# Layer 1's cross attention keeps x in SBUF for GEGLU; three tags of small tiles become one; two follower sweeps start earlier

## The chip, the cores and the metric

The program runs on one core of one Trainium2 chip. The metric is the device time of one execution in microseconds (us), lower is better. A core has five instruction streams that matter here: PE (the matmul engine; PEld are its weight loads), DVE (vector), ACT (activations), POOL (GpSimd) and SP, whose stream issues every DMA of this kernel. Each stream runs in its own order, and semaphores join them. SP's stream is one queue: an instruction on it that waits holds all that stand behind it.

## The reference

Four transformer layers run over x (32 batches of 112 rows and 256 columns) with a shared context (32 batches of 375 rows and 256 columns), in fp32:

```python
x = L0(x, ctx)   # cross attention, 16 query heads of 64 on 4 key heads, no residual
x = L1(x, ctx)   # quantised self attention, quantised cross attention, GEGLU
x = L2(x, ctx)   # cross attention with 16 heads of 64, ReLU feed-forward
x = L3(ctx, x)   # causal self attention, cross attention, ReLU feed-forward
```

Layer 1 is what the change is about. Its blocks each read the normalised x and add to x:

```python
h2 = _ln(x, ln2_g, ln2_b)
x = _attn(h2, context, a2_wq, a2_wk, a2_wv, a2_wo, a2_bo, d_q2, d_k2, d_v2, d_w2) + x
h3 = _ln(x, ln3_g, ln3_b)
hg = h3 @ ff_w1 + ff_b1
a, g = jnp.split(hg, 2, axis=-1)
x = a * jax.nn.gelu(g, approximate=False) @ ff_w2 + ff_b2 + x
```

In `_attn`, queries, keys and values are rounded to 8-bit steps, and so are the softmax's probabilities (16 heads of 16 columns).

## The kernel before

**Sweeps.** The nine blocks are sweeps over all 32 batches: l0x, l1s (self attention of layer 1), l1x (its cross attention), l1f (its GEGLU), l2x, l2f, l3s, l3x, l3f. Batches go in pairs (GB = 2). A sweep is a list of units (one per batch, or one per pair for a feed-forward), and a unit is a list of slots: l1x has 8 slots for a batch (two heads each), l1f 8 for a pair (one eighth of the hidden columns each). Work that prepares a unit (loads, norms, projections) is a list of atoms, each with a lead: so many slots of its own sweep ahead (LEAD, L79). Work that follows a slot (normalising the probabilities, their transpose, the values' matmul, the residual) comes so many slots behind it (LAGS, L67).

**Which sweeps run together.** PAIRS (L29) puts l1s beside l0x, l1f beside l1x, l3s beside l2f and l3f beside l3x. `order` (L1338) gives every slot a place on one axis, from which all slots are sorted. The second sweep of a pair starts `off` later:

```python
off = max(GB * dur + self.DELAY[s] * dur, done + self.GAP - t0) if q else 0.0
```

`dur` is the pair's nominal length of a batch (SPAN), `done` the place where the pair before ends. With DELAY = 3 l1s runs 5 batches behind l0x. The next pair starts at once when l0x's slots are through, so that l1x runs beside the last batches of l1s; l1f starts GAP = 30 units after l1s's last slot, some 9 batches behind l1x. l2x starts when l1f's slots are through. So the stages of the kernel's first half are: l0x alone, l0x with l1s, l1x with the rest of l1s, l1x with l1f, the rest of l1f alone, l2x.

**Order of instructions.** The Python above issues the work in that order with priorities; the Tile framework's scheduler then fixes the order on each engine, and takes the tiles' buffers from the free slots of their tags (BUFS, L64). A tag with `bufs=11` has 11 slots as large as its largest tile. An instruction whose tile finds no free slot waits for the last reader of an older one.

**x between sweeps.** `load_x` (L380) and `store_x` (L388) hand x over. Where `beside` (L373) is true, the later sweep of a pair takes the SBUF tile of the earlier one. For l1x and l1f it is not, since both stand in AGAIN (L378). Of every batch, l1x loads x (for the norm), loads it again for the residual (L1216), stores it to HBM (L396), and l1f loads it (L385), loads it again for its residual (L1294), and stores it: six DMAs of 112 KB on SP's queue.

**The small tiles.** Tag ki (6 slots of 1,504 bytes a partition) holds l1's rounding tiles (`fkq`, L893) and the rounded keys; ot (7 of 1,792) the attention outputs split in two parts, the rounded queries and the feed-forwards' hidden parts (L1271); pp2 (4 of 1,792) the four-head probabilities (L620), their transposes (L1185) and the masked queries of `queries_apart` (L884).

**The path of l1x's probabilities.** Score matmuls (L1111), row maxima (DVE, L606), exponentials (ACT, L612), reciprocal (DVE, L646), rounding (POOL and DVE, L213), clipping (DVE, L657), a DMA transpose issued from SP (L1130) four times a batch, then the matmuls with the values (PE, L1075) and the projection. The same sweep computes values of layer 2 ahead of time and stores them with four DMAs a batch (L502).

Of the kernel before, what the change touches and what calls it, by code (L numbers as in the profile page):

```python
# [8 lines left out]
F32 = mybir.dt.float32  # L9
# [51 lines left out]

class Kern:

    BUFS = dict(w=8, x=11, xh=4, ki=6, s1=9, sm=32, ot=7, pp2=4, k3=11, h=3, qs=2, k6=5)  # L64
    PBUFS = dict(sc=3, ps1=4, acc=1)

    LAGS = dict(  # L67
# [11 lines left out]
    LEAD = dict(  # L79
        l0x=dict(load=11, stats=10, apply=6, cload=11, cstats=8, cut=8, ctrans=5, q=4, k=[2, -2], v=-1),  # L80
        l1s=dict(load=5, stats=5, apply=3, q=2, k=2, v=1),
        l1x=dict(load=17, stats=12, apply=10, cload=14, cut=14, q=8, apart=[2, -1], k=4, v=-1, v2=[-2, -4, -6, -7], again=-7),
        l1f=dict(load=13, stats=11, apply=10, gate=2, gelu=1, again=-3),
        l2x=dict(load=10, stats=7, apply=6, cload=11, cut=7, q=4, k=[1, 1], v=0, vload=2),
        l2f=dict(load=6, stats=5, apply=3),
        l3s=dict(load=10, stats=8, apply=7, q=7, qload=3, k=6, v=3, c2=4, k2=1, v2=1),
# [288 lines left out]
        return any(self.sweeps[i : i + 2] == list(p) for p in PAIRS) and self.sweeps[i] not in self.AGAIN  # L375


    AGAIN = ("l1x", "l1f")  # L378

    def load_x(self, s, b):  # L380
        i = self.sweeps.index(s)
# [235 lines left out]
    def softmax4(self, sc, scale=None):  # L617

        nc = self.nc
        p = self.t([S, 4, S], F32, "pp2")  # L620
        sm = self.t([S, 4], F32, "sm")
        nm = self.t([S, 4], F32, "sm")
        nc.vector.tensor_reduce(nm, sc, AX.X, ALU.max, negate=True)
        if self.turn("exp4") == 1:
            nc.vector.tensor_tensor(p, sc, nm.unsqueeze(2).to_broadcast([S, 4, S]), ALU.add)
            nc.scalar.activation(p, p, AF.Exp, scale=1.0 if scale is None else scale)
            nc.vector.tensor_reduce(sm, p, AX.X, ALU.add)
            return p, sm
# [98 lines left out]
    def unit64(self, s, b0, i, qd, gb, W, g, cx, wd, wq, wk, wv, gqa, gkv, gvec, bvec):  # L727
# [33 lines left out]
        def mk(m):  # L761
            z = {}

            def a():
                qs = g["q", qd]
                scs = []
                for j in range(2):
                    sc = self.ps([S, 512], "sc")
                    scs.append(sc)
                    hd = 2 * m + j  # L770
                    kk = kv["k", qd // 2][:, qd % 2, :] if gqa else kv["k", m][:, j, :]
                    for q in range(2):
                        nc.tensor.matmul(sc[:, :TE], qs[:, hd, q, bs], kk, start=q == 0, stop=q == 1)  # L773
                z["p"], z["sm"] = self.softmax(scs, T)

            def b():
                if not gqa:
                    st["pt", m] = self.t([TB, 2, 3 * S], F32, "k3")
                elif m == 0:
                    pt = self.t([TB, 2, 2, 3 * S], F32, "k6")  # L780
                    st["pt"], st["pt", 0], st["pt", 1] = pt, pt[:, 0], pt[:, 1]
                self.transpose_p(z["p"], st["pt", m])

            def c():
                if m == 0:
                    return
                vq = kv["v"]
                av = self.ps([128, 2, S])
                for mm in range(1 if gqa else 2):
                    for a in range(3):  # L790
                        ta = slice(a * S, (a + 1) * S)
                        for j in range(2):
                            hd = qd if gqa else 2 * mm + j
                            o = av[64 * j : 64 * j + 64]
                            nc.tensor.matmul(  # L795
                                o if gqa else o[:, mm, :],
                                vq[:, a, hd * 64 : hd * 64 + 64],
                                st["pt"][:, :, j, ta] if gqa else st["pt", mm][:, j, ta],
                                start=a == 0,
                                stop=a == 2,  # L800
                            )
                ot = st["ot"] = self.t([128, 2, 2, S], F32R, "ot")
                self.copy("ohi", ot[:, 0], av)
                nc.vector.tensor_tensor(ot[:, 1], av, ot[:, 0].bitcast(F32), ALU.subtract)

            return Slot(a, lambda: self.normalise(z["p"], self.recip(z["sm"], 2), 2, T), b, c)
# [74 lines left out]

    def queries_apart(self, i, c, bs):

        t = self.t([128, 8, S], BF16, "pp2")  # L884
        self.nc.gpsimd.tensor_tensor(
            t,
            i[:, c, bs].unsqueeze(1).to_broadcast([128, 8, S]),
            self.own.unsqueeze(2).to_broadcast([128, 8, S]),
            ALU.mult,
        )  # L890
        return t

    def fkq(self, ps, inv, shape):  # L893

        nc = self.nc
        p = shape[0]
        f = self.t(shape, F32, "ki")
        self.scale("fk", f, ps, inv[:p], MAGIC)
        self.eng("clip").tensor_scalar(f, f, MAGIC + 127.0, MAGIC - 128.0, ALU.min, ALU.max)
        return f  # L900

    def qk_atoms(self, lead, w, src, W, isq, quant, prm, put, tag=None, keep=None, apart=False):
# [4 lines left out]
        def half(c):  # L907
            if quant and c == 0:
                both = isq and not apart
                z["i"] = self.t([128, 2, 2, W] if both else [128, 2, W], BF16, "ot" if isq else "ki")  # L910
            pq = self.ps([128, W])
            for k in range(2):
                self.mm3(pq, lambda i: w()[:, k, i, c * 128 : (c + 1) * 128], lambda i: src()(k, i), k == 0, k == 1)
# [91 lines left out]
    def unit16(self, s, b0, i, gb, g, wd, quant, self_attn, qb, kb, vb, dl, gvec, bvec):  # L1005
# [54 lines left out]
        def av(heads, pt, first, octets, ahead=True):  # L1060
# [21 lines left out]
                        )  # L1082
            if octets:
                if octets[0] == 0:
                    st["ot"] = self.t([128, 2, 2, S], F32R, "ot")
                oc = slice(octets[0], octets[-1] + 1)
                hi, lo = st["ot"][:, 0, oc, :], st["ot"][:, 1, oc, :]
                o = o[:, : len(octets), :]
                if quant:
                    self.scale("ohi", hi, o, dl["so"])  # L1090
                    nc.vector.scalar_tensor_tensor(lo, o, dl["so"], hi.bitcast(F32), ALU.mult, ALU.subtract)
                else:
                    bi = vb[:, octets[0] : octets[0] + 1]
                    self.shift("ohi", hi, o, bi)
                    nc.vector.scalar_tensor_tensor(lo, o, bi, hi.bitcast(F32), ALU.add, ALU.subtract)
# [52 lines left out]
        def quad(qd):  # L1148
# [28 lines left out]
            def b():  # L1177
# [4 lines left out]
                pst = self.ps([128, 4, S])  # L1182
                for j in range(4):
                    nc.tensor.transpose(pst[:S, j, :], z["p"][:, j, :], self.ident[:S, :S])
                z["pt"] = self.t([S, 4, S], F32, "pp2")  # L1185
                self.copy("copy", z["pt"], pst[:S])

            def c():
# [34 lines left out]
    def unitff(self, s, b0, gb, wd, gvec, bvec, b1, glu):  # L1223
# [33 lines left out]
        def mk(c):  # L1257
            z = {}

            def a():  # L1260
# [7 lines left out]
                    z["uu"] = uu  # L1268
                    return
                self.shift("relu", uu, pf, b1[:, c : c + 1], AF.Relu)  # L1270
                ul = z["ul"] = self.t([128, 2, W], F32R, "ot")  # L1271
                self.split(uu, ul[:, 0, :], ul[:, 1, :], ("upper", "lower"))

            def b():
# [85 lines left out]
        ev.sort(key=lambda e: e[:4])  # L1360
        return [(e[4], e[2], e[5]) for e in ev]

    DELAY = dict(l1s=3, l1f=5, l3s=3, l3f=3)
    GAP = 30.0
    PAUSE = 4
    OVER = dict(l2x=0.0, l3x=34.0)

# [232 lines left out]
```

## Time and profile before

| | us |
|---|---|
| three runs | 4955.44, 4955.54, 4960.33 (median 4955.54) |
| the profiled execution | 4969.08, of which the span of its instructions is 4967.3 |
| PE busy in the span | 4502.3 (91%) |
| DVE, ACT, POOL busy | 3625.6, 3409.2, 2112.1 |
| x loaded from HBM between sweeps (`x<-xd`) | 224 DMAs of 112 KB |
| x stored to HBM between sweeps (`xd<-x`) | 160 DMAs of 112 KB |

A row of a window below gives the stretch, its length, and then for PE, PEld, DVE, ACT and POOL the busy time and in brackets the number of instructions; after them the granted PE clock (1.00 is full), the mean busy share of the 16 DMA engines, and GB/s. Rows of waits give who waited for whom, the sum, how often, and the longest. Rows of a timeline give the start, the duration, the engine (SPq is SP's queue), the line, the operation, out<-in, and how many were merged. Line numbers are those of the kernel before.

### The profile page before, as it was taken

What the parts mean: (1) busy time and instruction counts of PE and PEld (TensorE: products, weight loads), DVE (VectorE), ACT (ScalarE), POOL (GpSimd) and SP (SyncE); (2) the same over time, 40 slices, a digit from 0 to 9 for tenths busy, and PEclk for the clock granted to TensorE, in tenths of its full rate; (3) what the DMA queues carried; (4) which work ended last, traced back from release to release, by engine and by line L of the source; (5) the groups of instructions that cost most, each with busy time, mean ns of one, the idle gap of its engine ahead of it and who ended that gap; (6) DMA issues with size and microseconds to landing.
All of it is one profiled execution on the core that took longest, in us unless ns stands there. A gap on an engine that the chain in (4) does not pass through costs nothing. (4 is left out here: it accounts for less than half of the span.)

```text
span 4967.3 us, 111690 instructions
## 1 busy us (share of the span) xinstructions
PE 4502.3 (91%) x37824; PEld 4010.3 (81%) x37824; DVE 3625.6 (73%) x9806; ACT 3409.2 (69%) x10644; POOL 2112.1 (43%) x3674
## 2 busy tenths in 40 slices
PE   5999999997778888888999999998998986899999
PEld 5888888886667777777999999997888886788878
DVE  4788888888887777776688888886555554677776
ACT  4788888887777766775577777774544544677776
POOL 4455555555443333332233333334333333566665
PEclk9999999999889999999999999999999998899999
DMA  4433333335666667667355555543656657666663
GB/s 102 124 85 86 84 80 88 86 87 127 135 141 134 138 128 135 129 143 143 110 142 143 142 142 143 143 128 108 196 172 198 189 182 212 174 160 165 160 165 85
DMA packets 585414, 674.53 MB, mean 136 GB/s; under 512 B 318688, under 2 KB 495056, under 8 KB 584656
## 3 DMA queue, kind: packets, MB, share of 16 engines
q1 hardware_dynamic: 584848, 667.40, 53.5%
q8 instruction: 305, 5.00, 0.4%
q14 instruction: 261, 2.14, 0.1%
HBM read 323.55 MB, written 173.02 MB: 100 GB/s over the span
## 5 line engine op out<-in xcount | busy, mean ns | idle before, releaser
L217 POOL TENSOR_SCALAR k<-k,sm 112x375 f32<-112x375 f32 (+1 forms) x1536 | 931.8, 619 | 1025.2 <-DVE sm L646 453.9
L200 ACT ACTIVATE k<-ps 125x336 f32<-125x336 f32 (+4 forms) x2005 | 912.8, 468 | 416.1 <-PE ps L237 190.1
L606 DVE TENSOR_REDUCE sm<-sc 112x1 f32<-112x375 f32 x1792 | 941.7, 539 | 151.8 <-PE sc L773 87.2
L612 ACT ACTIVATE k<-sc,sm 112x375 f32<-112x375 f32 x1536 | 879.5, 578 | 116.0 <-DVE sm L606 97.4
L664 PE MATMUL ps<-ident,k 112*125 112x112 f32 x4608 | 737.5, 277 | 19.8 <-issue 4.1
L664 PEld LDWEIGHTS ps<-ident,k 112*125 112x125 f32 x4608 | 649.9, 190 | 78.8 <-issue 41.8
L773 PE MATMUL sc<-k,qs 128*112 128x376 f32 x2048 | 540.0, 356 | 18.5 <-ACT k L612 8.3
L235 PE MATMUL ps<-w,k 128*125 128x256 f32 (+2 forms) x1344 | 435.6, 324 | 32.0 <-ACT k L612 17.9
L235 PE MATMUL ps<-h,w 128*128 128x224 f32 x1408 | 411.9, 300 | 44.0 <-DVE h L202 17.2
L695 DVE TENSOR_TENSOR k<-ps,k 64x376 fp32r<-64x376 f32 x640 | 350.0, 547 | 121.3 <-ACT k L200 106.0
L236 PE MATMUL ps<-h,w 128*128 128x224 f32 x1408 | 397.3, 284 | 0.7 <-DVE h L231 0.3
L237 PE MATMUL ps<-h,w 128*128 128x224 f32 x1408 | 395.0, 283 | 0.0
L236 PE MATMUL ps<-w,k 128*125 128x256 f32 (+2 forms) x1344 | 393.1, 292 | 0.0
L202 DVE COPY k<-ps 125x336 f32<-125x336 f32 (+2 forms) x619 | 289.0, 467 | 141.5 <-PE ps L237 65.2
L237 PE MATMUL ps<-w,k 128*125 128x256 f32 (+2 forms) x1344 | 391.9, 292 | 0.0
L235 PE MATMUL ps<-k,w 128*128 128x376 f32 x896 | 343.2, 383 | 37.2 <-DMA k<-cd 25.4
L213 POOL TENSOR_SCALAR k<-k,sm 112x375 f32<-112x375 f32 x256 | 164.5, 643 | 467.0 <-DVE sm L646 287.8
L795 PE MATMUL ps<-k,k 125*64 125x112 f32 (+1 forms) x4608 | 349.8, 296 | 3.7 <-DVE k L202 1.6
L773 PEld LDWEIGHTS sc<-k,qs 128*112 128x112 f32 x2048 | 304.4, 177 | 47.3 <-ACT k L612 23.5
L235 PEld LDWEIGHTS ps<-h,w 128*128 128x128 f32 x1408 | 275.0, 199 | 70.9 <-issue 28.9
L235 PEld LDWEIGHTS ps<-w,k 128*125 128x125 f32 (+2 forms) x1344 | 266.9, 199 | 72.7 <-ACT k L612 29.3
L612 ACT ACTIVATION_READ_ACCUMULATOR k<-sc,sm 112x1 f32 x1536 | 322.5, 210 | 0.0
(213 smaller groups left out, 12623.3 us busy)
## 6 DMA issues: line engine op xcount, KB each, us to landing
qs<-h SPq DMA_DIRECT2D x512, 224.0 KB
k<-k SPq DMA_DIRECT2D x192, 376.0 KB
k<-cd SPq DMA_DIRECT2D x64, 752.0 KB
vd<-k SPq DMA_DIRECT2D x128, 375.0 KB
k<-vd SPq DMA_DIRECT2D x128, 375.0 KB
qs<-dq_l3s SPq DMA_DIRECT2D x256, 112.0 KB
qs<-dq_l3x SPq DMA_DIRECT2D x256, 112.0 KB
x<-xd SPq DMA_DIRECT2D x224, 112.0 KB
```

Source lines behind the costliest of these rows:

```text
L200: self.nc.scalar.activation(out, in_, AF.Identity)
L202: self.nc.vector.tensor_copy(out, in_)
L217: self.nc.gpsimd.tensor_scalar(out, in_, by, 1.0, ALU.mult, ALU.mult)
L235: mm(out, lhs(0), rhs(0), start=start, stop=False)
L236: mm(out, lhs(0), rhs(1), start=False, stop=False)
L237: mm(out, lhs(1), rhs(0), start=False, stop=stop)
L606: nc.vector.tensor_reduce(nms[j], sc[j][:, :n], AX.X, ALU.max, negate=True)
L612: nc.scalar.activation(p[:, j, :n], sc[j][:, :n], AF.Exp, bias=nms[j], scale=1.0 if scale is None else scale, accum_out=sm[:, j : j + 1])
L664: self.nc.tensor.transpose(pst[:TB, a * S : (a + 1) * S], p[:, j, a * TB : (a + 1) * TB], self.ident[:S, :S])
L695: nc.vector.tensor_tensor(ks[o, j, :], pk[r, :TE], ks[r, j, :].bitcast(F32), ALU.subtract)
L773: nc.tensor.matmul(sc[:, :TE], qs[:, hd, q, bs], kk, start=q == 0, stop=q == 1)
L795: nc.tensor.matmul(o if gqa else o[:, mm, :], vq[:, a, hd * 64 : hd * 64 + 64], st["pt"][:, :, j, ta] if gqa else st["pt", mm][:, j, ta], ...
```

## The change

- AGAIN becomes empty. So `beside` is true for l1x and l1f: l1x adds its residual to the tile that it loaded for the norm, does not store x, and l1f takes that tile, adds to it, and stores it for l2x. Two DMAs of x a batch are left in the two sweeps.
- Tag x gets 14 slots for 11. Tags ki (6), ot (7) and pp2 (4) become one tag m with 14 slots of 1,792 bytes.
- l1s's DELAY is 2 for 3, and GAP 5 for 30: by the formula l1s runs 4 batches behind l0x, and l1f 7 batches behind l1x (the first operand of the `max` decides then, 154 units for 200).
- l1x's load of x has a lead of 14 slots for 17, l1f's of 11 for 13.

```diff
-    BUFS = dict(w=8, x=11, xh=4, ki=6, s1=9, sm=32, ot=7, pp2=4, k3=11, h=3, qs=2, k6=5)
+    BUFS = dict(w=8, x=14, xh=4, m=14, s1=9, sm=32, k3=11, h=3, qs=2, k6=5)
...
-        l1x=dict(load=17, stats=12, apply=10, cload=14, cut=14, q=8, apart=[2, -1], k=4, v=-1, v2=[-2, -4, -6, -7], again=-7),
-        l1f=dict(load=13, stats=11, apply=10, gate=2, gelu=1, again=-3),
+        l1x=dict(load=14, stats=12, apply=10, cload=14, cut=14, q=8, apart=[2, -1], k=4, v=-1, v2=[-2, -4, -6, -7], again=-7),
+        l1f=dict(load=11, stats=11, apply=10, gate=2, gelu=1, again=-3),
...
-    AGAIN = ("l1x", "l1f")
+    AGAIN = ()
...
-        p = self.t([S, 4, S], F32, "pp2")
+        p = self.t([S, 4, S], F32, "m")
...
-        f = self.t(shape, F32, "ki")
+        f = self.t(shape, F32, "m")
...
-                    st["ot"] = self.t([128, 2, 2, S], F32R, "ot")
+                    st["ot"] = self.t([128, 2, 2, S], F32R, "m")
...
-    DELAY = dict(l1s=3, l1f=5, l3s=3, l3f=3)
-    GAP = 30.0
+    DELAY = dict(l1s=2, l1f=5, l3s=3, l3f=3)
+    GAP = 5.0
```

The other lines with the tags ki, ot and pp2 (L799, L884, L910, L1185, L1271) change their tag in the same way.

More of the change, by code (lines that the diff above doesn't have):

```diff
@@ L801, in c @@
                             )
-                ot = st["ot"] = self.t([128, 2, 2, S], F32R, "ot")
+                ot = st["ot"] = self.t([128, 2, 2, S], F32R, "m")
                 self.copy("ohi", ot[:, 0], av)
@@ L882, in queries_apart @@
     def queries_apart(self, i, c, bs):
-        t = self.t([128, 8, S], BF16, "pp2")
+        t = self.t([128, 8, S], BF16, "m")
         self.nc.gpsimd.tensor_tensor(
@@ L909, in half @@
                 both = isq and not apart
-                z["i"] = self.t([128, 2, 2, W] if both else [128, 2, W], BF16, "ot" if isq else "ki")
+                z["i"] = self.t([128, 2, 2, W] if both else [128, 2, W], BF16, "m")
             pq = self.ps([128, W])
@@ L1184, in b @@
                     nc.tensor.transpose(pst[:S, j, :], z["p"][:, j, :], self.ident[:S, :S])
-                z["pt"] = self.t([S, 4, S], F32, "pp2")
+                z["pt"] = self.t([S, 4, S], F32, "m")
                 self.copy("copy", z["pt"], pst[:S])
@@ L1270, in a @@
                 self.shift("relu", uu, pf, b1[:, c : c + 1], AF.Relu)
-                ul = z["ul"] = self.t([128, 2, W], F32R, "ot")
+                ul = z["ul"] = self.t([128, 2, W], F32R, "m")
                 self.split(uu, ul[:, 0, :], ul[:, 1, :], ("upper", "lower"))
```

## The prediction

> **What bounds the kernel now.** The page's slices come first: PE is near full in l0x (to some 1150 us) and in l2x (2450 to 3350), and lower in between. So layer 1 is read by windows: l0x with l1s; l1x with the rest of l1s; l1x with l1f; l1f alone; l2x.
>
> ```profile
> span 4967.3 us, 111690 instructions
> PE   5999999997778888888999999998998986899999
> PEclk9999999999889999999999999999999998899999
> ```
>
> ```profile
> 300.00:1100.00 800.00, 775.02 (x6248) 663.34 (x6249) 659.91 (x1910) 697.30 (x2312) 414.02 (x844) 1.00 0.36 84
> 1150.00:1450.00 300.00, 228.53 (x1724) 188.93 (x1724) 260.13 (x702) 214.81 (x660) 134.07 (x248) 0.87 0.65 138
> 1500.00:2300.00 800.00, 694.94 (x5133) 614.98 (x5130) 600.30 (x1675) 558.25 (x1510) 283.61 (x434) 0.94 0.68 135
> 2322.00:2402.00 80.00, 76.64 (x436) 69.41 (x435) 35.16 (x97) 23.47 (x44) 15.93 (x26) 1.00 0.34 90
> 2450.00:3350.00 900.00, 896.34 (x7976) 846.28 (x7974) 738.51 (x1724) 651.86 (x1850) 292.85 (x496) 1.00 0.50 141
> ```
>
> The reader is to see that PE sets the pace in l0x with l1s (97% busy), in l1f alone (96%) and in l2x (99.6%), and no engine does while l1x runs: 76% and 87% for PE, 87% and 75% for DVE. By counts of l1x's score matmuls (L1111, 16 a batch) l1x takes 36.7 us a batch beside l1s (109 in 250 us from 1200) and 36.0 beside l1f (356 in 800 us from 1500). The much different companions leave its pace the same: it is set by something in l1x itself. Its waits from 1500 to 2300, PE's row and then SP's own:
>
> ```profile
> PE ps L1075 <- DMA k<-k: 63.6, 36, 4.7
> ```
>
> ```profile
> SPq L502 <- DVE k L202: 104.0, 37, 8.9
> SPq L385 <- DVE xh L441: 83.4, 21, 9.1
> SPq L385 <- DMA xd<-x: 81.6, 32, 6.2
> SPq L1130 <- POOL k L213: 63.0, 24, 4.1
> ```
>
> PE stands for 63.6 of its 105 idle us before the values' matmuls, until the transposed probabilities land. SP, which issues those transposes, stands 165 us for x alone: until a store of x has landed that the next load reads (81.6), and until the norm frees a slot of tag x (83.4). What that does to the transposes is in SP's timeline:
>
> ```profile
> 1752.56 3.53 SPq L1130 DMA_TRANSPOSE k<-k  x1
> 1756.70 1.00 SPq L552 DMA_DIRECT2D cd<-k  x1
> 1757.83 1.30 SPq L502 DMA_DIRECT2D vd<-k  x1
> 1760.58 10.21 SPq L385 DMA_DIRECT2D x<-xd  x3
> 1770.90 1.48 SPq L1130 DMA_TRANSPOSE k<-k  x1
> 1773.83 0.26 SPq L502 DMA_DIRECT2D vd<-k  x1
> 1774.15 0.32 SPq L385 DMA_DIRECT2D x<-xd  x1
> 1778.28 0.30 SPq L396 DMA_DIRECT2D xd<-x  x1
> 1778.67 1.36 SPq L1130 DMA_TRANSPOSE k<-k  x1
> ```
>
> A transpose that still waits for its data stands 3 to 5 us (1752.56); one whose data lay ready takes 1.4 (1770.90, right behind three loads of x that held the queue for 10.2 us). Going through the window like this, of 89 transposes 35 were short, and 30 of these stood behind loads or stores of x that had held the queue for more than 1 us. Those were late because of x.
>
> **The change part by part.** The sum is made against the profiled execution's 4969.1 us (13.5 above the median of the three runs, 4955.5, and 1.8 above its span) and then taken off the median. The built programs' orders give what is moved.
>
> *GEGLU's tail.* In PE's order 3.94 pairs of l1f stood behind l1x's last score before, and 2.94 after; the first gate comes after 6.1 batches of l1x, not 8.1. Alone, l1f did 248 of its matmuls at L1238 in 80 us (the window from 2322), 64 a pair: 20.6 us a pair, PE full. The pair moves into l1x's stage, where l1x's pace did not depend on its companion and PE is idle 13 to 24%. Taken: -20.6. Bounds: -20.6, and 0 if the moved PE work lengthens l1x as much. The tail is also when l2x's weights arrive; POOL's waits for these DMAs there (L204 on xh) were 4.6, 4.1 and 2.6 us in sum, of which none is counted and 11 kept for the range.
>
> *l1s one batch earlier.* 4.1 batches of l0x stand before its first score, not 5.1. So one batch of l0x changes from running alone to running with l1s: l0x's scores (L773, 32 a batch) were 107 in 100 us alone (29.9 us a batch) and 734 in 800 us with l1s (34.9). Both are PE-bound: +5.0. l1x loses that batch beside it. Counted 0, since l1x's pace did not change with its companion; it could give back up to the same 5.0.
>
> *The queue.* 96 loads and 32 stores of x go: two DMAs of x a batch are left of six. In SP's order from l1x's 41st to its 120th transpose (20 batches), 24 transposes stood directly behind a load and 6 behind a store of x before, and 10 and 0 after. What is late next is each transpose's own data (POOL's L213, 63.0 us in 24) and the store of layer 2's values (104.0, which stays). Bounds on the gain: 0, if those absorb it all, and all of PE's wait, 63.6 us for 22.25 batches, so 2.86 a batch, times the 25.9 batches that now run beside l1f: 74. I take half, 37: a third of the transposes was held by x, but those held were held long (10.2 us above), and the waits on data that remain are of 2 to 4 us and nearly as frequent.
>
> The Trainium skill's page "Perfetto Trace Analysis", section "Identifying the Most-Contended Engine", speaks against this step: DMA is to be judged by HBM utilization. At the 135 GB/s of l1x's window against the 358 a core of its section "Engine Utilization", DMA is far from full, and taking away 14 MB of transfers would be worth nothing; the forecast would then be 37 higher. I go by the queue's rows.
>
> *The clock.* l1x's windows were granted 0.87 and 0.94, the full stages 1.00. Less idle PE may raise it: 31.2 us of PE a batch (694.94 / 22.25) at 0.98 for 0.94 would be 1.3 us less, 33 over 25.9 batches. I count none and keep 33 for the range, because l3x's stage with 92% busy PE also shows only 0.96.
>
> The page "TensorE: Matmul & The Clock Gate", section "What's actually happening", says that the throttled state is the default and that activity releases it. By it fewer stalls before L1075 would pay twice, and part of the 33 would be added.
>
> *The tiles.* x gets room for l1f's lag: a tile lives from 14 slots (1.75 batches) ahead of l1x's pair until 1.25 batches (LAGS, 5 slots) after l1f's pair, 1.75 + 7 + 2 + 1.25 = 12 batches, and there are 14. Tag m loses three slots against the sum of the three, while l1x and l1s fill all of them (11.5 tiles a batch in l1x); layer 3, which used no ki, gains three. The trace names no wait for a slot of ki, ot or pp2 on PE; the nearest is x's own (83.4 us in 21 on SP, 4.0 each). 0 is taken; above, one such wait a batch (104 us) is the slower rival. The order in l2f with l3s and in l3x changes too (equal shares of PE's instructions in order 0.68 and 0.84; l2x's is the same): idle PE there was 10% and 8% of 600 us, and a tenth of it either way is some 11 us, kept for the range. ACT loads its tables twice more (13 to 14 each way, 1.28 us each): 2.6 us, hidden by ACT's 30% idle time.
>
> Sum: -20.6 + 5.0 - 37 = -52.6: 4916.5 for the profiled execution, 4903 for the median.
>
> **The rivals.**
>
> *Only the tail.* The transposes wait for their own data instead: -20.6 + 5.0, 4940. For it: 54 of 89 transposes waited for data anyway. Against it: 30 that did not.
>
> *All of the queue and the clock.* The 74 and the 33 come whole: 5.0 - 20.6 - 74 - 33 = -122.6, 4833. For it: no engine is full in l1x. Against it: DVE is at 75% and in a chain of four engines, and L502's 104 us stay on the queue.
>
> *Slower: too few slots in m.* Keys and queries of l1x hold slots over a batch or two, and the short rounding tiles (L897) queue behind them on ACT, with the exponentials behind those. It decides above 2.0 us a batch (52.6 / 25.9) that reach PE. At one wait of 4.0 us: +104, 5007. For it: 17 slots become 14 just where all three tags are used. Against it: the three tags could not lend to each other, and ACT has no such wait now.
>
> *Nothing changes in time.* The orders differ as described, so the change does what it says; its parts would have to cancel: 4955.
>
> **How the numbers follow.** Forecast 0.52 (its own range 4880 to 4930), only the tail 0.20, all of the queue and the clock 0.14, slower 0.10, cancelling 0.04. The measurement can tell about 0.2% (10 us) from no change. Faster: 0.52 + 0.17 + 0.14 = 0.83, with 0.03 of the tail's case within 0.2% because of the weights; same 0.03 + 0.04 = 0.07; slower 0.10. For 8 in 10 the range reaches half way into the case of 4833 and past that of 4940 by some 10 us for the later stages: 4850 to 4950.
>
> **What would show it.** Right: the stretch with l1f alone is some 60 us, not 80; l1x beside l1f takes 34 to 35 us a batch; PE's wait on the transposes falls to about 1.4 us a batch; SP's waits for x shrink to a few us. Wrong: PE's rows before L1075 stay and POOL or DVE is named by SP's transposes for what x held before; or ACT waits at L211 for a reader of m; or l3's stages move by more than 10 us.

## The result, and the profile after

The changed kernel took 4983.65 us (median; 4982.05 to 4996.02), the kernel before 4956.51 beside it. The ratio is 1.0048, with an interval from 1.0034 to 1.0062: slower by 0.5%, where 4903 and faster had been forecast. The profiled execution has a span of 4994.2 us for 4967.3.

The page after, its first line and two rows of slices:

```profile
span 4994.2 us, 111424 instructions
PE   6999999999778888888899999999999996899999
PEclk9999999999889999999999999999999998899999
```

The windows after (columns as explained with the profile before): l0x with l1s, l1x with the rest of l1s, l1x with l1f, l1f alone.

```profile
300.00:1150.00 850.00, 797.09 (x6200) 666.39 (x6198) 665.98 (x1903) 695.58 (x2299) 397.05 (x840) 0.99 0.36 78
1250.00:1450.00 200.00, 153.62 (x1101) 126.53 (x1098) 167.33 (x454) 141.07 (x435) 83.11 (x154) 0.83 0.64 129
1550.00:2350.00 800.00, 694.21 (x5209) 610.25 (x5208) 646.12 (x1704) 561.79 (x1526) 277.39 (x440) 0.96 0.73 124
2401.00:2461.00 60.00, 55.76 (x316) 50.28 (x316) 29.17 (x76) 18.42 (x35) 15.02 (x25) 1.00 0.35 91
```

PE is 94% busy in l0x with l1s, where it was 97%. In l1x with l1f it is 87% busy, as before, while DVE rose from 600.30 to 646.12 us of 800.

Where the time went is read best from the first and last start of each sweep's score matmuls. The rows of the lines L773 (l0x's scores) and L1163 (l1s's) up to 2000 us give engine, operation, out<-in, count, the shortest/median/longest duration in ns, and the first and last start. After:

```profile
L1163 PE MATMUL sc<-m,m x512: 204/210/338, 169.6 to 1457.2; 32*112 32x112 bf16 x171
L773 PE MATMUL sc<-k,qs x1024: 327/334/656, 55.0 to 1230.5; 128*112 128x376 f32 x171
```

Before:

```profile
L1163 PE MATMUL sc<-ki,ot x512: 204/210/338, 201.9 to 1430.3; 32*112 32x112 bf16 x171
L773 PE MATMUL sc<-k,qs x1024: 327/335/656, 55.9 to 1146.6; 128*112 128x376 f32 x171
```

l0x's last score comes 83.9 us later. The whole difference, by such starts:

| stretch | before | after | difference |
|---|---|---|---|
| start to l0x's last score | 1146.6 | 1230.5 | +83.9 |
| from there to l1x's last score | 1174.1 | 1168.7 | -5.4 |
| from there to l2x's first score (GEGLU's tail) | 95.1 | 76.3 | -18.8 |
| l2x's scores | 989.4 | 988.8 | -0.6 |
| from there to l3x's last score ("later") | 1521.3 | 1489.2 | -32.1 |

The sum is +27.0. Three of these are not what had been forecast: the large loss in l0x (+5.0 had been taken), the small gain in l1x (-37) and the gain in layer 3 (0).

### The profile page after: what moved, and what is told of

The parts are those of the page before. It is cut to its first block, busy times and chain, and to the rows that moved or that the text cites. A ratio compares the mean times of both kernels' runs of the same rounds, so it can differ in the third digit from the quotient of the medians.

```text
span 4994.2 us, 111424 instructions
## 1 busy us (share of the span) xinstructions
PE 4525.5 (91%) x37824; PEld 4007.3 (80%) x37824; DVE 3674.7 (74%) x9805; ACT 3408.1 (68%) x10646; POOL 2081.6 (42%) x3675
## 4 chain that ended last, share of the span: by engine, by line
PE 37%; DMA 7%; DVE 4%; ACT 1%; SPq 1%; issue 1%; POOL 1%; ACTq 0%; DVEq 0%; POOLq 0%
PE ps L664 6%; PE ps L235 5%; PE ps L236 4%; PE ps L237 4%; PE sc L773 3%; PE ps L795 3%; PE ps L1075 3%; DMA qs<-dq_l3s 2%; PE sc L1111 2%; PE acc L237 1%; PE acc L235 1%; PE acc L236 1%; DMA k<-cd 1%; DMA k<-dk 1%; DVE sm L606 1%
## 5 line engine op out<-in xcount | busy, mean ns | idle before, releaser
L217 POOL TENSOR_SCALAR k<-k,sm 112x375 f32<-112x375 f32 (+1 forms) x1536 | 918.3, 610 | 1077.7 <-DVE sm L646 487.2
L773 PE MATMUL sc<-k,qs 128*112 128x376 f32 x2048 | 544.0, 359 | 42.4 <-ACT k L612 26.2
L773 PEld LDWEIGHTS sc<-k,qs 128*112 128x112 f32 x2048 | 307.9, 178 | 83.7 <-ACT k L612 47.9
L213 POOL TENSOR_SCALAR k<-k,sm 112x375 f32<-112x375 f32 x256 | 155.9, 609 | 518.2 <-DVE sm L646 354.4
L795 PEld LDWEIGHTS ps<-k,k 125*64 125x64 f32 x4608 | 250.5, 138 | 87.2 <-ACT k L200 22.4
```

Of the source, the lines that this page charges most:

```text
L217: self.nc.gpsimd.tensor_scalar(out, in_, by, 1.0, ALU.mult, ALU.mult)
L795: nc.tensor.matmul(o if gqa else o[:, mm, :], vq[:, a, hd * 64 : hd * 64 + 64], st["pt"][:, :, j, ta] if gqa else st["pt", mm][:, j, ta], ...
```

## The experiments

The table has one profiled execution of each kernel, cut in the same way, and the timed ratio to the kernel before. Executions of one kernel lie some 14 us or more apart (the changed kernel's from 4982.05 to 4996.02, of which the longest is the profiled one), so a few us in one stretch say little. For l0x+l1s the table itself gives a measure: before, h3_seven_apart and j1_pp2_six have the same order of PE's instructions up to 1130 us and lie between 942.1 and 944.7; e3_only_tags, f1_tags16, f3_seven_odd and f4_seven_x13_m15 share another order and lie between 977.9 and 981.2. "l0x+l1s" runs from l1s's first score to l0x's last; in brackets it is divided by the batches in it (26.9 at 5 batches behind, 27.9 at 4, 25.9 at 6). "l1x" runs from l0x's last score to l1x's last. p is the tile of the four-head probabilities (L620); the masked queries of l1x (L884) take the tag of layer 1's p in every kernel.

| kernel | l1s, GEGLU behind | p of layer 1; 3 | l0x+l1s | l1x | tail | later | ratio [interval] |
|---|---|---|---|---|---|---|---|
| before | 5, 9 | pp2; pp2 | 944.7 (35.1) | 1174.1 | 95.1 | 1521.3 | 1 |
| after | 4, 7 | m; m | 1060.9 (38.0) | 1168.7 | 76.3 | 1489.2 | 1.0048 [1.0034, 1.0062] |
| e1_delay3 | 5, 8 | m; m | 978.1 (36.4) | 1255.2 | 82.9 | 1458.4 | 1.0116 [1.0100, 1.0132] |
| e2_only_delay2 | 4, 9 | pp2; pp2 | 1027.0 (36.8) | 1164.5 | 97.9 | 1516.8 | 1.0090 [1.0071, 1.0110] |
| e3_only_tags | 5, 9 | m; m | 979.2 (36.4) | 1179.6 | 95.2 | 1464.3 | 0.9999 [0.9989, 1.0009] |
| e4_reload | 4, 7 | m; m | 1057.1 (37.9) | 1190.9 | 77.7 | 1460.4 | 1.0066 [1.0054, 1.0078] |
| f1_tags16 | 5, 9 | m; m | 979.1 (36.4) | 1183.9 | 94.7 | 1462.8 | 1.0000 [0.9985, 1.0015] |
| f2_delay4 | 6, 9 | m; m | 980.1 (37.9) | 1198.9 | 97.8 | 1464.2 | 1.0046 [1.0030, 1.0062] |
| f3_seven_odd | 5, 7 | m; m | 977.9 (36.4) | 1181.1 | 76.1 | 1461.9 | 0.9922 [0.9902, 0.9943] |
| f4_seven_x13_m15 | 5, 7 | m; m | 981.2 (36.5) | 1179.3 | 75.7 | 1470.6 | 0.9934 [0.9908, 0.9959] |
| g1_pp2_apart | 5, 9 | pp2; pp2 | 937.3 (34.9) | 1181.2 | 95.1 | 1510.5 | 0.9980 [0.9962, 0.9998] |
| g2_ki_apart | 5, 9 | m; m | 958.3 (35.7) | 1176.0 | 95.4 | 1472.5 | 0.9951 [0.9930, 0.9972] |
| h1_seven_pp2 | 5, 7 | pp2; pp2 | 937.7 (34.9) | 1171.8 | 75.9 | 1507.9 | 0.9944 [0.9920, 0.9967] |
| h3_seven_apart | 5, 7 | pp2; pp2 | 942.1 (35.1) | 1166.1 | 75.8 | 1522.8 | 0.9949 [0.9934, 0.9964] |
| h4_pt_in_m | 5, 7 | pp2; pp2 | 937.5 (34.9) | 1178.5 | 75.8 | 1523.5 | 0.9971 [0.9954, 0.9989] |
| h5_p_and_pt_in_m | 5, 7 | pp2; m | 935.8 (34.8) | 1174.0 | 75.4 | 1462.6 | 0.9845 [0.9820, 0.9870] |
| j1_pp2_six | 5, 9 | pp2; pp2 | 943.2 (35.1) | 1193.9 | 94.5 | 1519.7 | 1.0042 [1.0025, 1.0060] |
| k1_tags_clip_dve | 5, 9 | m; m | 981.3 (36.5) | 1193.6 | 95.5 | 1465.4 | 1.0006 [0.9988, 1.0025] |
| k2_best_clip_dve | 5, 7 | pp2; m | 945.5 (35.2) | 1184.3 | 75.6 | 1458.5 | 0.9880 [0.9852, 0.9909] |
| k3_before_clip_pool | 5, 9 | pp2; pp2 | 932.2 (34.7) | 1174.0 | 95.1 | 1523.5 | 0.9964 [0.9948, 0.9980] |

### The parts of the change one by one

*The changed kernel with l1s's offset put back*; by the formula of `order`, GEGLU then runs 8 batches behind.

```diff
-    DELAY = dict(l1s=2, l1f=5, l3s=3, l3f=3)
+    DELAY = dict(l1s=3, l1f=5, l3s=3, l3f=3)
```

> The changed kernel with l1s's DELAY back at 3, so l1s runs 5 batches behind l0x again (GEGLU then follows 8 batches behind, since GAP counts from l1s's end). In the changed kernel the stretch from l1s's first score to l0x's last took 1060.9 us for 27.9 batches (38.0 each), before 944.7 for 26.9 (35.1 each). Theory A (the offset between l0x and l1s): 5 batches is odd, so the work that each sweep does once for a pair of batches falls into alternate batches, at 4 it falls into the same one; this stretch comes back to about 945 us, the total to about 4983.7 - 84 + 10 for the half pair more of GEGLU alone = 4910. Rival B (the one tag m with 14 slots for 17 slows l0x with l1s): it stays at some 38 us a batch and the total near 4985.

*The kernel before with l1s's offset alone changed* (GAP keeps GEGLU 9 behind).

```diff
-    DELAY = dict(l1s=3, l1f=5, l3s=3, l3f=3)
-    GAP = 30.0
+    DELAY = dict(l1s=2, l1f=5, l3s=3, l3f=3)
+    GAP = 64.0
```

> The kernel before with l1s's DELAY 2 alone; GAP 64 keeps GEGLU where it was. Theory A (offset): the stretch from l1s's first score to l0x's last goes from 35.1 to about 38 us a batch, the total to about 4957 + 80 = 5037. Rival B (tag m): 35.1 a batch stays, 5 us for one batch more of both, total 4955 to 4965.

*The kernel before with the tags alone merged.*

```diff
-    BUFS = dict(w=8, x=11, xh=4, ki=6, s1=9, sm=32, ot=7, pp2=4, k3=11, h=3, qs=2, k6=5)
+    BUFS = dict(w=8, x=11, xh=4, m=14, s1=9, sm=32, k3=11, h=3, qs=2, k6=5)
...
-        p = self.t([S, 4, S], F32, "pp2")
+        p = self.t([S, 4, S], F32, "m")
```

> The kernel before with the three tags merged into m (14 slots) alone; x keeps 11 slots and the reload. Theory A: l0x with l1s stays at 35.1 us a batch, and the gain that the changed kernel shows between l2x's last score and l3x's last score (1521.3 to 1489.2 us) comes here, since layer 3 had 11 slots of ot and pp2 and now has 14: total about 4957 - 32 = 4925. Rival B: l0x with l1s slows to 38 a batch, total about 4957 + 78 - 32 = 5003. If the later gain is due to x's 14 slots instead, the later stretch stays at 1521.

*The changed kernel with the handover alone undone.*

```diff
-    AGAIN = ()
+    AGAIN = ("l1x", "l1f")
```

> The changed kernel with the reload of x back (AGAIN as before), everything else as changed. If the handover is worth what PE waited for late transposes, l1x (1164 us from its first to its last score in the changed kernel) gets 30 to 40 us longer and the total about 5020. If the transposes wait for their own data in any case (the changed kernel took 359 scores of l1x in 800 us, before 356), l1x stays within 10 us and the total within 4980 to 4995.

Two parts cost time in l0x with l1s, and each does so alone. The offset alone brings l0x's last score from 1146.6 to 1198.6 (+52.0), the tags alone to 1184.8 (+38.2). Together that is 90, and the changed kernel has 83.9. The handover has no share in it: without it the stretch is 1057.1 for 1060.9.

The first run puts l1s back and is still slower, for another reason. Its l1x lasts 1255.2 us. From 1600 to 2400 us, in that run's l1x with l1f, a row of SP's waits, one of PE's, and one row of SP's timeline:

```profile
SPq L385 <- DMA xd<-x: 57.6, 15, 6.1
PE ps L443 <- DVE xh L441: 37.0, 10, 3.7
```

```profile
1903.27 6.71 SPq L385 DMA_DIRECT2D x<-xd  x2
```

An x tile lives 1.75 + 8 + 2 + 1.25 = 13 batches at 8 behind, for which 14 slots hardly suffice: loads of x stand on SP for a slot that a store must clear, the transposes stand behind them, and PE stands 37.0 us for the norm of x. At 7 behind (f3_seven_odd) l1x takes 1181.1, and that row of PE has 1.0 us in the same window. But 8 is also the only even offset of GEGLU in the table; no run has 8 behind with more slots of x, so slots and parity are not told apart here.

### An even offset makes two heavy batches coincide

Why does one batch of offset cost 52 us? One batch more runs together, at 35.1 us for 30: +5. The rest, 47 us, is 1.7 us in each of 27.9 batches. Batches go in pairs, and both sweeps have work that comes once a pair (the projections of two batches at once). The idea: with an odd offset the two sweeps' heavy batches alternate, with an even one they coincide. Windows of 25 us of the run with the offset alone (columns as above; POOL's busy time is the fifth):

```profile
500.00:525.00 25.00, 22.26 (x179) 18.52 (x178) 21.79 (x64) 22.47 (x80) 18.56 (x38) 1.00 0.56 106
525.00:550.00 25.00, 24.50 (x195) 21.01 (x195) 20.10 (x55) 19.55 (x60) 8.80 (x22) 1.00 0.26 58
550.00:575.00 25.00, 23.75 (x190) 19.84 (x186) 18.44 (x58) 20.91 (x73) 8.66 (x19) 1.00 0.46 105
575.00:600.00 25.00, 22.85 (x178) 19.18 (x177) 21.11 (x64) 22.13 (x77) 18.88 (x38) 0.93 0.35 79
600.00:625.00 25.00, 24.36 (x191) 20.42 (x189) 17.64 (x49) 20.08 (x64) 7.66 (x18) 1.00 0.24 56
```

The same windows of the kernel before:

```profile
500.00:525.00 25.00, 24.67 (x192) 20.98 (x192) 20.02 (x58) 21.28 (x67) 10.13 (x22) 1.00 0.35 79
525.00:550.00 25.00, 24.89 (x211) 21.95 (x210) 21.88 (x67) 22.07 (x75) 15.10 (x28) 1.00 0.35 86
550.00:575.00 25.00, 24.30 (x195) 20.00 (x196) 21.02 (x61) 23.66 (x85) 14.00 (x33) 1.00 0.44 101
575.00:600.00 25.00, 24.76 (x200) 21.29 (x197) 21.74 (x58) 20.05 (x64) 10.73 (x23) 1.00 0.27 61
600.00:625.00 25.00, 24.61 (x212) 21.57 (x210) 20.90 (x65) 22.30 (x76) 13.80 (x27) 1.00 0.45 109
```

At 4 behind POOL is busy 18.6 of 25 us, then 8.8 and 8.7, then 18.9 again: a beat of 75 us, two batches of 36.8. PE falls to 22.3 and 22.9 in the heavy windows. At 5 behind POOL stays between 10.1 and 15.1, and PE between 24.3 and 24.9. If this is parity, 6 behind must be as bad as 4:

```diff
-    DELAY = dict(l1s=2, l1f=5, l3s=3, l3f=3)
-    GAP = 5.0
+    DELAY = dict(l1s=4, l1f=5, l3s=3, l3f=3)
+    GAP = -4.0
```

(on the changed kernel, with the reload of x and its leads as before)

> m with 14 slots, x with 14, the reload, l1s 6 batches behind l0x (DELAY 4; GAP -4 keeps GEGLU at 200 units). At 5 behind with m=14 l0x with l1s took 36.4 us a batch, at 4 behind 37.9 (the run with the reload back). If an even offset is what costs (both sweeps do their work for a pair of batches at once), 6 behind takes about 37.9 too. If nearness costs (l1s's chain, or slots held), 6 behind takes 36.4 or less.

It took 37.9 us a batch, as at 4 behind (37.9 and 38.0) and not as at 5 (36.4) with the same tags. The beat is there too:

```profile
550.00:575.00 25.00, 22.84 (x188) 19.05 (x187) 20.21 (x63) 22.19 (x77) 11.96 (x24) 1.00 0.51 110
575.00:600.00 25.00, 21.98 (x173) 17.94 (x173) 21.22 (x62) 22.46 (x74) 15.94 (x35) 0.98 0.36 71
600.00:625.00 25.00, 24.87 (x189) 20.99 (x186) 16.44 (x45) 15.85 (x51) 6.60 (x17) 0.95 0.24 57
```

With the same tags at 5 behind (e3_only_tags) POOL is busy 11.0 to 14.2 us in every window of 25 from 500 to 700. So for the three offsets that ran, parity decides and not nearness. Which instructions make a batch heavy was not taken apart. The practical test is the whole change with l1s 5 and GEGLU 7 behind (GAP keeps the 7), and the same with the slots shared out otherwise:

```diff
-    DELAY = dict(l1s=2, l1f=5, l3s=3, l3f=3)
-    GAP = 5.0
+    DELAY = dict(l1s=3, l1f=5, l3s=3, l3f=3)
+    GAP = -16.0
```

> The changed kernel with l1s 5 behind l0x (DELAY 3) and GAP -16, so that GEGLU is 7 behind l1x as in the change, not 8 as in the run with DELAY 3 alone, where l1x took 1248.7 us against 1164.4. If x's 14 slots were too few for 8 behind, l1x takes 1165 to 1175 here; l0x with l1s 978 as there; GEGLU's tail 76; the total about 4984 - 50 = 4934, less up to 28 if the later stages come out as in the run with the tags alone. If l1x is slow because of l1s at 5 behind, it stays near 1250 and the total near 5010.

```diff
-    BUFS = dict(w=8, x=14, xh=4, m=14, s1=9, sm=32, k3=11, h=3, qs=2, k6=5)
+    BUFS = dict(w=8, x=13, xh=4, m=15, s1=9, sm=32, k3=11, h=3, qs=2, k6=5)
```

(with the same DELAY and GAP)

> As the run with GEGLU 7 behind and l1s 5 behind, but x with 13 slots and m with 15. If slots of m limit l0x with l1s, that stretch falls from 978 to about 962; if x needs 14 slots for GEGLU 7 behind (12 batches live), l1x gets longer than 1175; if 12 are enough it does not. Total 4890 to 4930 if neither x nor the order turns against it.

Both beat the kernel before, by 0.8% and 0.7%. Two numbers of the change, l1s's DELAY and the GAP that goes with it, made the difference between a gain and a loss; DELAY alone (e1_delay3) made it worse.

### The merged tag: not the number of slots

Too few slots was the forecast's slower rival. Merged tags with 16 slots for 14:

```diff
-    BUFS = dict(w=8, x=11, xh=4, m=14, s1=9, sm=32, k3=11, h=3, qs=2, k6=5)
+    BUFS = dict(w=8, x=11, xh=4, m=16, s1=9, sm=32, k3=11, h=3, qs=2, k6=5)
```

> The kernel before with one tag m of 16 slots (x keeps 11, the reload and the offsets stay). With m=14 alone l0x with l1s took 36.4 us a batch (979.2 us for 26.9) against 35.1 before, and the stretch from l2x's last score to l3x's last 1464 against 1521. If the number of slots (14 for 17) is what slows l0x with l1s, 16 slots bring it to 35.1 to 35.5 (about 950), and the total to 4957 - 57 + 5 = 4905. If sharing itself does it, by another order of the instructions, it stays at 36.4 and the total at about 4957.

979.1 for 979.2 (and 981.2 with 15 in f4_seven_x13_m15). The number of slots is not it. PE's order in l0x is the same with 14, 15 and 16 slots, and another one than with three tags. So which of the three tags must stay apart?

```diff
-    BUFS = dict(w=8, x=11, xh=4, ki=6, s1=9, sm=32, ot=7, pp2=4, k3=11, h=3, qs=2, k6=5)
+    BUFS = dict(w=8, x=11, xh=4, m=12, s1=9, sm=32, pp2=4, k3=11, h=3, qs=2, k6=5)
```

(ki and ot merged, pp2 apart)

> The kernel before with ki and ot merged (m, 12 slots) and pp2 left alone with 4; nothing else. With all three merged, l0x with l1s took 36.4 us a batch whether m had 14, 15 or 16 slots, 35.1 with the tags apart; and the stretch from l2x's last score to l3x's last 1464 against 1521. If pp2's four slots are what holds l1s's softmax back in a good way, l0x with l1s takes 35.1 here, and if they are what holds layer 3 back, the later stretch stays at 1521: total about 4957. If merging ki with ot is what matters, l0x with l1s takes 36.4 and the later stretch 1521 or 1464.

```diff
-    BUFS = dict(w=8, x=11, xh=4, ki=6, s1=9, sm=32, ot=7, pp2=4, k3=11, h=3, qs=2, k6=5)
+    BUFS = dict(w=8, x=11, xh=4, ki=6, m=11, s1=9, sm=32, k3=11, h=3, qs=2, k6=5)
```

(ot and pp2 merged, ki apart)

> The kernel before with ot and pp2 merged (m, 11 slots) and ki left alone with 6. If pp2's four slots matter in both places, l0x with l1s takes 36.4 us a batch and the later stretch 1464: total about 4957. If the later gain needs more than 11 slots, that stretch stays above 1500.

With pp2 apart the loss is gone (937.3); with ki apart some 40% of it stays (958.3 against 944.7). In every run of the table with l1s 5 behind the stretch goes with the tag of layer 1's probabilities: 932 to 946 us in the nine with p in pp2, 958 to 981 in the seven with p in a shared tag.

POOL's rows of waits from 250 to 1130 us seemed to say why: POOL stands at L899, the clip of l1s's rounding, for ACT's rounding before it. With all tags merged:

```profile
POOL m L899 <- ACT m L211: 99.5, 43, 3.7
```

With pp2 apart:

```profile
POOL m L899 <- ACT m L211: 38.4, 28, 3.7
```

It was 79.9 with ki apart and 55.2 in the kernel before, so the wait and the stretch (99.5 and 979, 38.4 and 937, 79.9 and 958, 55.2 and 945 us) went together. What stands behind it on POOL is the normalising of l0x's probabilities. Three kernels test that. Two take all of l1s's clips from POOL, with merged tags and in the fastest kernel (below); the third gives POOL all of them in the kernel before:

```diff
-        ("l1s", "clip"): (0, 1, 1), ("l1s", "vcopy"): (0, 1, 0), ("l1s", "round"): (0, 1, 1), ("l1s", "rest"): (0, 1, 3),
+        ("l1s", "clip"): (0, 1, 0), ("l1s", "vcopy"): (0, 1, 0), ("l1s", "round"): (0, 1, 1), ("l1s", "rest"): (0, 1, 3),
```

> The kernel with only the tags merged (14 slots of m), and layer 1's self attention takes the clips of its rounding (L899) all to DVE instead of by turns to DVE and POOL. From 250 to 1130 us POOL stood at L899 for ACT's L211 for 99.5 us in 43 where the tags were merged, 100.3 with 16 slots, 79.9 with only the keys' tag apart, 55.2 in the kernel before and 38 to 38.4 in three kernels with the four-head probabilities apart; 26.9 batches of l0x beside l1s took 979, 979, 958, 945 and 936 to 938 us. Theory: the merged tag puts the clips earlier in POOL's order, POOL stands there for data, and the normalising of l0x's probabilities behind it comes late. With no clip on POOL the stretch falls from 979 to 930 to 945 us, and the time from 4961.5 to 4915 to 4935. Rival: the two only go together, and the order costs elsewhere: the stretch stays at 970 to 985 and the time at 4950 to 4970, or longer because DVE has 17 us more to do.

> The fastest kernel so far (x handed over, GEGLU 7 batches behind, l1s 5, probabilities of layer 1 in pp2, of layer 3 in m) with the same edit of the clips. POOL stood 38.0 us at L899 there. Theory: the stretch goes from 936 to 915 to 930 us and the time from 4884 to 4865 to 4878. Rival: it stays at 930 to 945, and the time at 4880 to 4895.

```diff
-        ("l1s", "clip"): (0, 1, 1), ("l1s", "vcopy"): (0, 1, 0), ("l1s", "round"): (0, 1, 1), ("l1s", "rest"): (0, 1, 3),
+        ("l1s", "clip"): (0, 0, 1), ("l1s", "vcopy"): (0, 1, 0), ("l1s", "round"): (0, 1, 1), ("l1s", "rest"): (0, 1, 3),
```

> The kernel before with the clips of layer 1's self attention all on POOL: the wait doubled. Theory: POOL stands 90 to 120 us at L899 instead of 55, the stretch goes from 945 to 965 to 985 us and the time from 4956 to 4975 to 5000. Rival: POOL has idle time enough (414 of 800 us busy); the stretch stays at 935 to 955 and the time within 10 us of 4956.

The forecasts of the theory fell in all three. With no clip on POOL the merged kernel has 981.3 us for 979.2, and the fastest one 945.5 for 935.8. The third kernel's wait rose only to 65.3 us, not to 90 to 120, and its stretch is 932.2 for 944.7. So the clips on POOL are not what costs. But POOL is not cleared by this, for its wait went to another line. POOL's row at L213, the rounding of l1s's probabilities, in the same window, with the tags merged, and then with the clips on DVE as well:

```profile
POOL m L213 <- DVE sm L646: 133.2, 73, 4.4
```

```profile
POOL m L213 <- DVE sm L646: 219.2, 75, 7.9
```

The two rows L899 and L213 together have 232.7 us with the tags merged, 219.2 with the clips on DVE, 184.2 in the kernel before (129.0 of them at L213) and 165.4 in the third kernel (100.1). They still go with the stretches (979, 981, 945, 932 us); only the fastest kernel does not fit, where they fell from 168.1 to 156.3 us while the stretch grew. That merging the tags costs some 38 us of l0x is shown, and that the number of slots is not the reason. That it comes by the other order of the instructions is the likely way. What in that order costs the time is open, and POOL's standing for l1s stays a suspect.

### Layer 3 gains from the same tag

The later stretch goes the other way: 1458 to 1489 us wherever layer 3's p is in a shared tag, 1508 to 1524 wherever it is in pp2. So the best of both puts layer 1's p into pp2 and layer 3's into m, with the handover and 5 and 7 batches. On the way there, the handover with pp2 apart, and with all three tags apart:

```diff
-    BUFS = dict(w=8, x=14, xh=4, m=14, s1=9, sm=32, k3=11, h=3, qs=2, k6=5)
+    BUFS = dict(w=8, x=13, xh=4, m=11, pp2=4, s1=9, sm=32, k3=11, h=3, qs=2, k6=5)
...
-        p = self.t([S, 4, S], F32, "m")
+        p = self.t([S, 4, S], F32, "pp2")
```

> As the run with GEGLU 7 behind, l1s 5 behind and x with 13 slots, but pp2 apart with 4 slots and m (ki and ot) with 11. If pp2's four slots are good for l0x with l1s and bad for layer 3: l0x with l1s 945, the later stretch 1521, l1x 1174, tail 76, so about 4957 - 19 = 4938. If only one of the two holds, 4900 or 4975.

```diff
-    BUFS = dict(w=8, x=11, xh=4, ki=6, s1=9, sm=32, ot=7, pp2=4, k3=11, h=3, qs=2, k6=5)
+    BUFS = dict(w=8, x=14, xh=4, ki=5, ot=6, pp2=4, s1=9, sm=32, k3=11, h=3, qs=2, k6=5)
...
-    AGAIN = ("l1x", "l1f")
+    AGAIN = ()
```

> The handover (x with 14 slots, GEGLU 7 behind, l1s 5 behind) with the three tags apart: ki 5, ot 6, pp2 4 (one less of ki and ot than before). l0x with l1s 35.1 us a batch (945) if it is sharing that costs, later stretch 1521 or worse for the slot of ot less, tail 76: total 4935 to 4950. If one slot less of ki or ot costs by itself, l0x with l1s or l1x is longer.

Then only the transposed probabilities of layer 3 into m, and then p too:

```diff
-                z["pt"] = self.t([S, 4, S], F32, "pp2")
+                z["pt"] = self.t([S, 4, S], F32, "m")
```

> As the run with the handover, GEGLU 7 behind, l1s 5 behind, pp2 apart with 4 slots and m (ki and ot) with 11, but layer 3's transposed probabilities (L1185) take slots of m; layers 0 to 2 keep the same tags. If pp2's four slots hold layer 3 back through these two tiles a quad, the stretch from l2x's last score to l3x's last falls from 1508 towards 1465, and l0x with l1s stays at 938: total about 4936 - 40 = 4896. If the later gain is an accident of the order, it stays near 1508 and the total at 4936.

```diff
-        p = self.t([S, 4, S], F32, "pp2")
+        p = self.t([S, 4, S], F32, "m" if scale is None else "pp2")
```

> The same with layer 3's probabilities (L620 there) in m as well, so that pp2 serves layer 1 alone. m then has 11 slots for all of layer 3, as in the run with ki apart (1472). If pp2's slots matter: l0x with l1s 938, the later stretch 1465 to 1475, total about 4900. If four more slots for layer 3 (15 in the run before this one) count, it is the slower of the two.

And the kernel before with six slots of pp2, at ot's expense:

```diff
-    BUFS = dict(w=8, x=11, xh=4, ki=6, s1=9, sm=32, ot=7, pp2=4, k3=11, h=3, qs=2, k6=5)
+    BUFS = dict(w=8, x=11, xh=4, ki=6, s1=9, sm=32, ot=5, pp2=6, k3=11, h=3, qs=2, k6=5)
```

> The kernel before with pp2 6 slots and ot 5 (for 4 and 7), tags apart. If the number of pp2's slots decides how far l1s's softmax runs ahead, l0x with l1s goes from 35.1 us a batch towards 36.4 (944.7 to between 950 and 979) and the later stretch from 1521 towards 1464, with no tag merged. If only sharing a tag does it, both stay (945 and 1521), or suffer from ot.

The transposes alone bring nothing (later 1523.5), two more slots of pp2 nothing (1519.7), p in m 61 us (1462.6). Most of it lies in l3s: from l2x's last score to l3s's last score it is 834.6 us with p in pp2 and 780.9 with p in m; l3x differs by 7. PE's rows of waits from 3450 to 4050 us with only the transposes in m:

```profile
PE ps L235 <- DMA k<-cd: 40.1, 10, 5.6
PE sc L1163 <- DMA qs<-dq_l3s: 5.5, 3, 2.4
```

And with p in m too:

```profile
PE sc L1163 <- DMA qs<-dq_l3s: 18.5, 12, 2.4
PE ps L235 <- DMA k<-cd: 4.7, 2, 4.3
```

In these rows PE stands 45.6 us for loads in the one and 23.2 in the other. Scaled from 600 us to l3s's length that is, as an estimate, a little over half of the 54 us; whether p needs more slots than six, or just other neighbours in the order, is not settled.

With p in m for layer 3 and in pp2 for layer 1, the kernel took 4883.88 us, a ratio of 0.9845 [0.9820, 0.9870]. It beats the kernel before by 1.55% and the changed one by 2.0%.

## Why the prediction was wrong, step by step

*"GEGLU's tail. Taken: -20.6"* held where it was looked for: 95.1 to 76.3, so -18.8. But the pair that left the tail seems not to have been free in l1x. With the reload l1x takes 1190.9 at 7 behind. The offset of l1s alone changes l1x by -9.6 (1164.5), the tags alone by +5.5 (1179.6). If these add up, e4_reload's +16.8 leaves 20.9 (16.8 + 9.6 - 5.5) for the pair together with x's slots and leads. That would be the step's own other bound, 0, "if the moved PE work lengthens l1x as much". Where the pair's move and the handover come together, l1x hardly changes: 1181.1 for 1179.6 (f3_seven_odd, e3_only_tags) and 1166.1 for 1174.1 (h3_seven_apart, before). With the tail's 19 us that makes the two steps together worth some 18 and 27 us, not 58.

*"l1s one batch earlier. Both are PE-bound: +5.0"* is the largest failure. The step priced the one batch that joins the others, and took the pace of those for given. At 4 behind each of the 27.9 batches that run together takes 1.7 us longer, and l0x's last score comes 52.0 us later (e2_only_delay2), of which l1x gave back 9.6 (up to 5.0 had been allowed). The step went by an average of 97% busy PE at 5 behind, and whether two offsets are alike was never asked; at 4 behind the beat of 75 us shows in short windows. (Its 734 scores in 800 us are 732 in the trace, which moves the term by 0.1.)

*"The queue. I take half, 37"* was too much. The changed kernel against the one with only the reload back: l1x 1168.7 for 1190.9, so 22.2, and the estimate of 20.9 for the pair takes that up. SP's five largest rows and PE's row of waits after, 1550 to 2350:

```profile
SPq L502 <- DVE k L202: 211.7, 67, 6.8
SPq L1130 <- POOL k L213: 45.6, 18, 4.4
SPq L1130 <- PE ps L1238: 37.2, 7, 6.4
SPq L1130 <- PE ps L237: 35.9, 6, 6.8
SPq L385 <- DMA xd<-x: 31.0, 13, 3.2
```

```profile
PE ps L1075 <- DMA k<-k: 49.5, 34, 4.5
```

The waits for x fell from 165 us to 31, and L502's store of layer 2's values, which "stays", doubled from 104.0 to 211.7: SP was freed to wait for the next thing in its queue. Not all of that is the handover's doing. With the reload back, and x's 14 slots and the changed offsets kept (e4_reload, same window), the wait for x is already down to one row:

```profile
SPq L385 <- DMA xd<-x: 59.6, 25, 3.6
```

The forecast had also read this row as a load that waits for the store whose x it reads. In the changed kernel that cannot be: l1x's loads there read what l1s had stored by 1493 us. Before, the store that ended such a wait had been issued 2 to 7 us earlier, with GEGLU 9 batches behind. So SP most likely stood for a slot of tag x that the store had to clear, in both rows for x and not in one of them.

SP's timeline after:

```profile
1705.67 6.89 SPq L1130 DMA_TRANSPOSE k<-k  x1
1717.66 0.25 SPq L502 DMA_DIRECT2D vd<-k  x1
1718.01 4.23 SPq L1130 DMA_TRANSPOSE k<-k  x1
1726.99 0.25 SPq L502 DMA_DIRECT2D vd<-k  x1
```

These transposes stand 4 to 7 us with no load of x before them, and between 1712.6 and 1717.7 SP stands before L502. Of 90 transposes 78 took over 2.1 us, and 10 of the 12 short ones stood behind x; before, it was 54 of 89, and 30 of the 35 short ones. They wait for the probabilities in part; the two rows that name PE, which has no part in making these, may be waits for a slot, and the record does not settle it. PE's wait fell by 14 of 63.6 us, to 2.2 a batch and not 1.4. With the reload back it is 51.1, so nearly all of that fall came without the handover, and by which way the handover gave its 22.2 us this row does not show. l1x beside l1f made 359 scores in 800 us for 354 (the forecast had counted 356): 35.7 us a batch for 36.2, not 34 to 35. The rule that the forecast weighed and left, in the Trainium skill's page "Perfetto Trace Analysis", section "Identifying the Most-Contended Engine" (judge DMA by HBM utilization), came out nearer to l1x's total here, at 124 GB/s after and 135 before. Yet undoing the handover alone, at 131 GB/s, cost l1x 22.2 us, for which such a reading would give nothing.

*"The clock. I count none"* stands: 0.96 for 0.94 in l1x with l1f, and no gain of l1x with it.

*"The tiles. 0 is taken"* failed twice: +38 in l0x with l1s, and -57 in layer 3 (the tags alone, 1464.3 for 1521.3), where "some 11 us" had been kept. In the changed kernel layer 3 gained only 32.1; that it moved by more than 10 us was one of the forecast's own signs of being wrong. The 25 us more than with the tags alone are not explained; with the reload back it has 1460.4, and part of the difference can be the execution (the profiled one of the changed kernel was 12 us above its median, that of e4_reload 5 below). The step read slots and waits for slots. With the tag the scheduler built another order, and that order was compared by its share of equal rows and not priced.

*The slower rival* had the sign and not the mechanism: two more slots change nothing, and the loss is in l0x and not in l1x. *"Only the tail"* was right in that the transposes still waited with x out of their way. Parts of both signs had been given 4 in 100, as cancelling; there were such parts, -24 in l1x and the tail and -32 in layer 3, but +84 in l0x outweighed them.

## What to carry to other kernels

When two pipelined sweeps that work in pairs share a core, try an odd and an even offset (here 5 was fast, 4 and 6 slow), and look at their stretch in windows of about a third of the period, since averages hide the beat. A wait that grows along with a slow order is a suspect and no more: take it away, and then look where the waiting went, since with the clips gone POOL's wait stood at the next line. A queue that is freed of one wait goes on to the next; price what stands behind it before the gain is counted.

## What the runs showed of the hardware

One VectorE instruction changed its length with what GpSimd did. The rounding of l1x's probabilities on DVE, the group row of the changed kernel's page (busy us, mean ns, idle before):

```profile
L213 DVE TENSOR_SCALAR k<-k,sm 112x375 f32<-112x375 f32 x256 | 214.1, 836 | 0.0
```

The kernel before:

```profile
L213 DVE TENSOR_SCALAR k<-k,sm 112x375 f32<-112x375 f32 x256 | 172.9, 675 | 0.0
```

Such an instruction takes 0.41 us undisturbed. In the changed kernel's timelines of POOL and DVE, around 1603 us:

```profile
1603.77 3.32 POOL L885 TENSOR_TENSOR m<-m,ownb 128x896 bf16<-128x896 bf16 x2
```

```profile
1603.48 3.82 DVE L213 TENSOR_SCALAR k<-k,sm 112x375 f32<-112x375 f32 x1
1607.22 0.34 DVE L899 TENSOR_SCALAR m<-m 128x376 f32<-128x376 f32 x1
```

DVE's 0.41 us became 3.82 and ended 0.21 us after POOL's two masked copies of the queries (L885, 1.68 us each). From 1260 to 2400 us 37 of DVE's L213 took over 0.9 us, 94.1 us in all. Of these 30 (86.8 us) overlapped an L885, and 25 ended within 0.4 us of its end. In the kernel before it was 36 (58.2 us), 24 of them beside an L885 (42.6 us). The mean goes with the tag again, 651 to 710 ns with layer 1's p in pp2 and 738 to 944 with p in a shared tag. The changed kernel has two L885 directly in a row 13 times, the kernel before twice; that is not all of it, since j1_pp2_six has 26 such pairs at 651 ns. The Trainium skill's page "SBUF — State Buffer", section "SBUF: two separate sides", says that the two engines share one pair of ports, locked for a whole instruction, so that the loser stands. The rows agree, and show that the loser can stand through two instructions. By the records VectorE's instruction started first here, 0.29 us before GpSimd's, and was the one that stood. What this costs l1x was not measured by itself.
